# A window-attention and Fourier kernel: the sync queue's transfers moved from a scheduler's order to the program's order

## The chip, the cores and the metric

The kernel runs on one core of a Trainium2 chip. The metric is the device time of one launch in microseconds, the median of several runs. The core has five engines with a queue each: TensorE (PE in the profile; PEld is its weight load), VectorE (DVE), ScalarE (ACT), GpSimd (POOL) and SyncE (SP). In this kernel SP computes nothing. It issues nearly all of the transfers between memory and the on-chip buffers, in the order of its queue, each after the semaphores it waits for.

## The reference

32 images of 56x56 positions and 128 channels, in float32, go through two layers; each is added to its input.

```python
x = x + window_attention(_gn(x), rpb_table, w_qkv, w_proj, b_proj)
x = x + fourier_mlp(_gn(x), w0, w1, W1, b1, W2, b2)
# _gn: normalisation over 32 groups of 4 channels, per image

# window attention: shift by 3, cut into 64 windows of 7x7, 4 heads of 32
qkv  = (win @ w_qkv.T)
attn = softmax(q * scale @ k.T + bias + mask)
out  = (attn @ v) @ w_proj.T + b_proj          # windows back to rows, shift back

# fourier_mlp, 32 modes of 56 along each axis
xy = idct(einsum('bixy,ioy->boxy', dct(x, axis=W)[..., :32], w0))
xx = idct(einsum('bixy,ioy->boxy', dct(x, axis=H)[..., :32], w1))
b  = relu((xx + xy) @ W1 + b1) @ W2 + b2       # 128 -> 512 -> 128
```

## The kernel before, in words

**Cycles.** An image has 8 rows of windows, and the kernel runs in cycles of one such row, 8 to an image. In a cycle it starts the attention of one row (queries, keys, scores), does the values and the projection of the row begun three cycles earlier, and beside these a slice of the Fourier layer of the previous image or of the one before that. `fourier(cycle)` says which slice: the slice numbers c run from 0 to 15 for an image and begin 11 cycles after its first row. Below, i is the number of the cycle modulo 8, so i=0 starts a new image on the attention side.

**Orders.** PE, ACT, DVE and POOL run their instructions as the program writes them: the whole main part stands in a `manual_schedule` over these four. SP is in a second, inner `manual_schedule` only through the prologue (the first image's loads and the first 11 cycles, `first_rows`). In the main loop the scheduler of the library places SP's instructions, by its own estimate of when each can go, among the others.

**Quarters.** The next image comes in as four quarters of 32 rows by 28 columns, called (k, u) in the code. `load_quarter` (lines 145 to 157) issues four DMAs of 112 KB for one; from the third image on all four quarters use one buffer, `xin`. `turn_quarter` (lines 339 to 361) transposes it on DVE (L351, L353, L354 or L356) into the window layout. It is called at the head of a cycle, in `next_quarter`, for (0,0) in i=0, (1,0) in i=4 and (1,1) in i=5; and for (0,1) in the middle of i=0, in `next_groups`. `next_begin` (line 1222), in the second half of a cycle, loads the quarter that the next cycle begins with. The load of (0,1), the "late" one of `next_steps`, stands in `next_quarter` behind the turn of (0,0).

**What follows a turn on DVE.** In i=0 the order on DVE is: sums of the projection's output (L662), turn of (0,0), sums of squares (L683), the copy of the value bias out of PSUM (L433), the even or odd half of the values' output (L622), the two additions of bias and mask to the scores (L506), the row maximum (L516), the turn of an attention block (L575), the turn of (0,1), the row sums (L528, L530), the last addition of the feed-forward (L939), the addition of the projection (L645). PE needs four attention banks `pa` in rotation; L433, L622, L506 and L645 are what frees them, besides ACT.

**The other transfers of the main loop.** Tokens `xr` of a row (`load_tokens`, L132), stores of the attention's result `scr` (L653), columns `htok` (L790), mode stores `zscr` (L813) and mode loads `zT` (`load_modes`, L824, two buffers; called by `load_back` for the next cycle), the residual `res` of a feed-forward group (`ff_in`, L875 and L880, two buffers), which POOL adds a bias to (L892) and DVE adds the result to (L939), and the output (L955, L956, L963, L970).

Of the kernel before, what the change touches and what calls it, by code (L numbers as in the profile page):

```python
# [11 lines left out]
F32 = mybir.dt.float32  # L12
# [4 lines left out]
P = 128  # L17
S = 56
# [3 lines left out]
NH = 4  # L22
HD = C // NH
WT = WS * WS
# [11 lines left out]
JP = 64  # L36
# [9 lines left out]
CONV_BEGIN = NWR + 3  # L46
# [4 lines left out]
def swin_fourier_kernel(  # L51
# [20 lines left out]
    nc = tc.nc  # L72
# [258 lines left out]
    def image_begin(b):  # L331
        im = Image()
        im.b = b
        im.half, im.xw, im.xr, im.eT = {}, {}, {}, {}
        return im
# [27 lines left out]
    def copy_wrap(im, copy):  # L363
        a, b = (
            t[:, : NWR * WS * n].rearrange("p (j h s) -> p j h s", j=NWR, s=WS)
            for t, n in zip((im.half[0], im.half[1]), ROWS)
        )
        copy(b[:, :, KB:], a[:, :, :SS])
# [500 lines left out]
    def ff_in(im, g):  # L869
        t0, n = sum(FF_GROUPS[:g]), FF_GROUPS[g]  # L870
        k, last = n // P, n % P
        xff = im.xf.rearrange("p r w -> p (r w)")
        scr_tok = im.scr.rearrange("h w c -> (h w) c")
        res = work.tile([P, 4, C], F32, tag="res", name="res")
        nc.sync.dma_start(  # L875
            res[:, :k], scr_tok[t0 : t0 + k * P].rearrange("(n p) c -> p n c", p=P)
        )
        if last:
            for hs in HALVES:
                nc.sync.dma_start(res[hs, k, :JP], scr_tok[t0 + k * P : t0 + n, hs])  # L880
        im.res = res
        im.hid = []
        for f in range(NF):
            ph = conv_bank()
            halved(ph[:, :n], wff1[:, f * P : (f + 1) * P], xff[:, t0 : t0 + n])
            hf = work.tile([P, HB], F32, tag="hid", name="hid", bufs=NF)
            nc.scalar.activation(hf[:, :n], ph[:, :n], AF.Relu, bias=b1sb[:, f : f + 1])  # L887
            im.hid.append(hf)
# [135 lines left out]
    def halves_first(cycle):  # L1024
        begins = [im for im, c in fourier(cycle) if c == 0]
        last, j = row(cycle - 4)
        if cycle % NWR == NWR - 1:
            norm_step(cycle)
        tokens_bias(cycle)
        im, i = row(cycle)  # L1030
        behind_short = im and i == NWR - 1
        if behind_short:
            attn_q(im, i)
            attn_exp(cycle - 1)
        if cycle == CONV_BEGIN or (cycle - 1) % NWR not in EARLY:
            divide(cycle)
        if last and cycle > CONV_BEGIN:
            attn_sums(last, j)
        next_quarter(cycle)
        if im:  # L1040
            if not behind_short:
                attn_q(im, i)
            attn_k(im, i)
            if i == NWR - 2:
                wrap_rows(cycle)
        late = im and i in LATE_SQUARES
        if last and cycle > CONV_BEGIN and not late:
            attn_squares(last, j)
            sum_squares(last, j)
        if not late:  # L1050
            next_tokens(cycle)
        if cycle % NWR == 0:
            norm_step(cycle)
        for im, c in fourier(cycle):
            if c in FF_AT:
                ff_in(im, FF_AT.index(c))
        for im in begins:
            start_stats(im)

# [112 lines left out]
    def next_quarter(cycle):  # L1172
        b, quarter, late, _ = next_steps(cycle)
        if quarter:
            turn_quarter(images[b], *quarter)
        if late and (b, *late) not in xins:
            xins[(b, *late)] = load_quarter(b, *late)

# [53 lines left out]
    def first_rows(cycle):  # L1232
        im, i = row(cycle)
        im3, i3 = row(cycle - 3)
        if cycle > 3:
            next_tokens(cycle)
        if im:
            attn_q(im, i)
            attn_k(im, i)
        if cycle == NWR:  # L1240
            norm_step(cycle)
        last, j = row(cycle - 4)
        if last:
            attn_sums(last, j)
        if cycle >= NWR:
            next_quarter(cycle)
        if cycle:
            attn_exp(cycle - 1)
        if im3:
            attn_values(im3, i3, cycle - 3, True)  # L1250
        tokens_bias(cycle)
        if im:
            attn_scores(im, i, cycle)
            attn_max(cycle)
        if last:
            attn_squares(last, j)
            sum_squares(last, j)
            add_sums(last, j)
        divide(cycle)
        turn(cycle)  # L1260
        if im3:
            attn_project(im3, i3)
        if cycle in (0, NWR - 1):
            norm_step(cycle)
        if im:
            attn_v(im, i, cycle)
        if cycle == 0:
            for half in range(2):
                bias_and_mask(nc.vector, 1, 1, half)
        next_begin(cycle)  # L1270
        if cycle < NWR:
            next_quarter(cycle)
        if cycle == NWR - 2:
            wrap_rows(cycle)
        next_groups(cycle)
        if cycle == NWR - 2:
            for _ in range(2):
                norm_step(NWR - 1)
        if cycle in (3, 5):
            back_weights(cycle // 2 - 1)  # L1280
        if cycle == 6:
            ff_weights()
        if cycle == CONV_BEGIN - 1:
            attn_sums(im3, i3)
            attn_squares(im3, i3)
            sum_squares(im3, i3)
            attn_exp(cycle)

    ET = mybir.EngineType
    with tc.manual_schedule(engines={ET.PE, ET.Activation, ET.DVE, ET.Pool}):  # L1290
        with tc.manual_schedule(engines={ET.SP}):
            images[0] = image_begin(0)
            for k in range(2):
                for u in range(2):
                    turn_quarter(images[0], k, u)
                if k:
                    copy_wrap(images[0], nc.vector.tensor_copy)
                for u in range(2):
                    xins[1, k, u] = load_quarter(1, k, u)
                for i in range(NP * k, NP * k + NP):  # L1300
                    row_stats(images[0], i)
            for i in range(2):
                load_tokens(images[0], i)
            for m in range(8):
                mix_weights(m)
            for _ in range(3):
                norm_step(-1)
            for r, t in ((0, 0), (0, 1), (1, 0)):
                for half in range(2):
                    bias_and_mask(nc.vector, r, t, half)  # L1310
            extra = big.tile([P, S, S], F32, tag="xf", name="a_extra", bufs=2)
            extra = extra.rearrange("p r w -> p (r w)")[:, : AT + JP - WT]
            nc.gpsimd.memset(extra[:, AT:], 0.0)
            a_ends.append(extra)
            a_sb.append(extra[:, :AT].rearrange("p (t w j) -> p t w j", t=NH, w=NP))
            for cycle in range(CONV_BEGIN):
                first_rows(cycle)
        for cycle in range(CONV_BEGIN, NB * NWR + CONV_BEGIN + FF_AT[-1] - NWR + 1):
            halves_first(cycle)
            if not row(cycle - 3)[0]:  # L1320
                eighths(cycle)
                for r in range(2):
                    columns_turn(cycle, r)
                behind_max(cycle)
                quarters(cycle)
                last_fetch(cycle)
                half_columns(cycle)
                half_columns(cycle, True)
                scale_first(cycle, 0)
                scale_first(cycle, 1)  # L1330
                load_first(cycle)
                last_out(cycle)
                load_back(cycle + 1)
                continue
            if not has_ff(cycle):
                half_columns(cycle)
            eighths(cycle)
            early = any(c == 10 for _, c in fourier(cycle))
            if early:
                columns_turn(cycle, 0)  # L1340
            quarters(cycle)
            if row(cycle)[0]:
                attn_max(cycle)
            if not early:
                columns_turn(cycle, 0)
            columns_turn(cycle, 1)
            last_fetch(cycle)
            if row(cycle)[0] and cycle % NWR in LATE_SQUARES:
                sum_squares(*row(cycle - 4))
                next_tokens(cycle)  # L1350
            behind_max(cycle)
            load_first(cycle)
            halves_last(cycle)
# [62 lines left out]
```

## Time and profile before

| what | value |
|---|---|
| median of 3 runs | 3230.74 us (3228.96 to 3234.39) |
| the profiled execution, its own time | 3231.41 us |
| its span, first to last instruction | 3229.6 us |
| granted TensorE clock, mean | 0.994 |
| PE / DVE / POOL / ACT busy | 3145.1 / 2517.3 / 2297.7 / 2184.8 us |
| data moved | 448.47 MB, mean 139 GB/s |
| DMA issues of the quarters (`xin`) | 480 of 112 KB |
| DVE idle before L351 for a quarter, 400 to 3000 us | 66.0 us in 51 waits |

A row of the timeline reads: start, duration in us (from the first to the last of merged instructions), engine, line, operation, output<-input with shapes, count, and in brackets the idle time of the engine before it with what ended it. For SP a row is the time in which DMAs are issued; the data land later. A row of the waits reads: engine, line, waited for what, us in total, times, longest. Windows give for a stretch the busy time of each engine, the granted clock, the busy share of the 16 DMA engines and GB/s.

### The profile page before, as it was taken

The page shows a single profiled execution, that of the slowest core. Times are in us where ns is not written, and L with a number is a line of the kernel's source. Part 1 is how long each engine was busy: PE and PEld are TensorE (multiplying, and loading weights), DVE is VectorE, ACT ScalarE, POOL GpSimd, SP SyncE. Part 2 cuts the span into 40 slices and gives each one's busy share as a digit, 9 for nine tenths or more (in the row PEclk, how much of TensorE's full clock was granted, in tenths as well). Part 3 has the DMA queues.
Part 4 walks back from the last instruction along what each step waited for, and adds up shares of the span by engine and source line. Part 5 has one row for each costly group of instructions (what it writes and reads, how often), then busy time and mean ns, then how long its engine had stood idle before and what let it go on. Part 6 is the DMA issues. An engine that isn't in the chain of part 4 may idle for free.

```text
span 3229.6 us, 152033 instructions
## 1 busy us (share of the span) xinstructions
PE 3145.1 (97%) x65664; PEld 2348.3 (73%) x65664; DVE 2517.3 (78%) x4764; ACT 2184.8 (68%) x4004; POOL 2297.7 (71%) x2570
## 2 busy tenths in 40 slices
PE   5789999999999999999999999999999999999999
PEld 4567777777777777777777777777777777777776
DVE  7678887888887888887888887888888888888751
ACT  4466777666777676776676777666776666777664
POOL 5467777777777777777777777777777777777741
PEclk9899999999999999999999999999999999999999
DMA  7446566656566655566656566556656656565443
GB/s 128 96 118 146 140 141 147 140 143 146 136 143 146 144 141 142 141 143 144 144 138 145 140 144 145 143 137 145 143 141 145 148 135 146 143 143 142 123 137 103
DMA packets 1171652, 448.47 MB, mean 139 GB/s; under 512 B 527690, under 2 KB 1141116, under 8 KB 1170980
## 3 DMA queue, kind: packets, MB, share of 16 engines
q1 hardware_dynamic: 1162788, 437.41, 56.9%
q8 instruction: 514, 8.42, 1.2%
q10 hardware_dynamic: 7584, 1.18, 0.3%
q14 instruction: 158, 1.29, 0.1%
q0 software_dynamic: 608, 0.17, 0.0%
HBM read 277.00 MB, written 161.48 MB: 136 GB/s over the span
## 4 chain that ended last, share of the span: by engine, by line
PE 95%; POOL 1%; DVE 1%; ACT 1%; issue 1%; DMA 1%; SPq 0%; DVEq 0%; ACTq 0%; POOLq 0%
PE pc L124 41%; PE pa L124 10%; PE pa L476 8%; PE pc L803 7%; PE pa L498 6%; PE pa L637 6%; PE pa L592 6%; PE pc L842 5%; PE pc L756 4%; PE pc L563 1%; PE pc L929 0%; ACT k L463 0%; PE pa L703 0%; POOL a L517 0%; DMA zT<-zscr 0%
## 5 line engine op out<-in xcount | busy, mean ns | idle before, releaser
L547 POOL TENSOR_TENSOR blocks<-a,rs 32x272 f32<-32x272 f32 (+3 forms) x1434 | 1219.6, 858 | 384.9 <-DVE rs L530 274.6
L124 PE MATMUL pc<-wff,hid 128*64 128x128 f32 x12288 | 713.1, 273 | 1.6 <-issue 0.6
L124 PE MATMUL pc<-xf,wff 128*64 128x512 f32 (+2 forms) x3584 | 714.5, 539 | 0.0
L124 PEld LDWEIGHTS pc<-wff,hid 128*64 128x64 f32 x12288 | 680.0, 137 | 8.4 <-issue 4.2
L517 POOL TENSOR_TENSOR a<-a,mx 128x784 f32<-128x784 f32 x250 | 376.6, 1507 | 294.8 <-DVE mx L516 269.3
L124 PEld LDWEIGHTS pc<-xf,wff 128*64 128x64 f32 x3584 | 263.7, 136 | 370.3 <-issue 295.7
L887 ACT ACTIVATE hid<-pc,b1sb 128x512 f32<-128x512 f32 (+2 forms) x896 | 500.6, 642 | 41.9 <-PE pc L124 41.6
L124 PE MATMUL pa<-xw,wn 128*64 128x392 f32 x2048 | 392.5, 498 | 29.1 <-ACT wn L429 28.5
L506 DVE TENSOR_TENSOR a<-pa,bm 128x392 f32<-128x392 f32 x500 | 259.0, 560 | 168.2 <-PE pa L498 155.5
L483 ACT COPY v<-pa 128x512 f32<-128x512 f32 x256 | 152.0, 594 | 283.7 <-PE pa L476 275.1
L463 ACT ACTIVATE k<-pa,bqkv,heads 128x392 f32<-128x392 f32 x512 | 318.9, 674 | 15.3 <-ACT q L450 1.1
L138 POOL TENSOR_TENSOR xr<-xr,bproj 128x384 f32<-128x384 f32 (+1 forms) x256 | 292.9, 1144 | 47.2 <-DMA xr<-in_x_dram 24.5
L892 POOL TENSOR_TENSOR res<-res,b2sb 128x512 f32<-128x512 f32 (+1 forms) x224 | 252.1, 1126 | 77.7 <-DMA res<-scr 57.1
L778 ACT ACTIVATE y<-modes,rstd 128x448 f32<-128x448 f32 x256 | 276.6, 1138 | 41.8 <-DVE modes L771 31.4
L450 ACT ACTIVATE q<-pa,bqkv 128x392 f32<-128x392 f32 x256 | 149.8, 585 | 229.0 <-PE pa L124 227.2
L523 ACT ACTIVATE a<-a 128x784 f32<-128x784 f32 x250 | 214.0, 856 | 130.3 <-POOL a L517 130.0
L575 DVE STREAM_TRANSPOSE eT<-blocks 128x1024 f32<-128x1024 f32 x240 | 295.1, 1230 | 0.0
L592 PEld LDWEIGHTS pa<-eT,v 49*32 49x32 f32 x16384 | 173.0, 106 | 157.9 <-issue 70.8
L528 DVE TENSOR_REDUCE sm<-a 128x16 f32<-128x784 f32 x250 | 239.8, 959 | 56.0 <-ACT a L523 55.9
L476 PE MATMUL pa<-wn,xw 128*64 128x128 f32 x4096 | 281.8, 279 | 1.6 <-issue 1.2
L516 DVE TENSOR_REDUCE mx<-a 128x16 f32<-128x784 f32 x250 | 242.2, 969 | 7.7
L476 PEld LDWEIGHTS pa<-wn,xw 128*64 128x64 f32 x4096 | 219.8, 137 | 36.6 <-issue 2.3
(126 smaller groups left out, 4978.6 us busy)
## 6 DMA issues: line engine op xcount, KB each, us to landing
zscr<-z SPq DMA_DIRECT2D x512, 112.0 KB
xin<-in_x_dram SPq DMA_DIRECT2D x480, 112.0 KB
htok<-scr SPq DMA_DIRECT2D x128, 392.0 KB
zT<-zscr SPq DMA_DIRECT2D x192, 256.0 KB
res<-scr SPq DMA_DIRECT2D x160, 256.0 KB
out_dram<-res SPq DMA_DIRECT2D x160, 256.0 KB
scr<-x SPq DMA_DIRECT2D x256, 112.0 KB
xr<-in_x_dram SPq DMA_DIRECT2D x256, 84.0 KB
```

The lines of the kernel that those rows point to most:

```text
L124: nc.tensor.matmul(dst[ps], lhsT=lhsT[:, ps], rhs=rhs, start=start, stop=stop)
L138: nc.gpsimd.tensor_tensor(piece, piece, bproj.unsqueeze(1).to_broadcast([P, n, C]), ALU.add)
L463: nc.scalar.activation(k_sb[:, u], pk[:, :RT].rearrange("p (w j) -> p w j", j=WT), AF.Identity, bias=im.bias[:, 3 + u : 4 + u], scale=head ...
L476: nc.tensor.matmul(pv[HALVES[w % 2], w // 2 * C : (w // 2 + 1) * C], lhsT=im.half[i // NP][:, t0 : t0 + JP], rhs=im.w[:, 2 * C : 3 * C], s ...
L506: nc.vector.tensor_tensor(a[:, 2 * hp : 2 * hp + 2, :, 0:WT].rearrange("p u w j -> p w u j"), ps[hp][:, :RT].rearrange("p (w u j) -> p w u ...
L517: nc.gpsimd.tensor_tensor(a3, a3, mx.unsqueeze(2).to_broadcast([P, 2 * NWR, WT]), ALU.subtract)
L547: nc.gpsimd.tensor_tensor(dst[to, k, :, :n], a3[src, :, kb * KB : kb * KB + n], rs[src].unsqueeze(2).to_broadcast([src.stop - src.start, 2 ...
L575: nc.vector.transpose(eT.rearrange("p t (k j) -> p k t j", k=2), blocks[r % 2])
L592: nc.tensor.matmul(po4[u][h * HD : (h + 1) * HD, pr], lhsT=v[ks, pr, h * HD : (h + 1) * HD], rhs=eT[ks, h * NP + pr, :WT], start=True, sto ...
L778: nc.scalar.mul(y[:, r], t.rearrange("p (n k) -> p n k", k=NM), im.rstd)
L887: nc.scalar.activation(hf[:, :n], ph[:, :n], AF.Relu, bias=b1sb[:, f : f + 1])
L892: nc.gpsimd.tensor_tensor(im.res[:, :k], im.res[:, :k], b2sb.unsqueeze(1).to_broadcast([P, k, C]), ALU.add,)
```

## The change

The two blocks of `manual_schedule` become one over all five engines, and the main loop is inside it. So SP runs its transfers in the program's order in the main loop too. The lines of the prologue move one level to the left and are otherwise the same. The load of the late quarter becomes a function of its own, `late_quarter`. In the prologue's cycles it is called where it was; in a cycle of the main loop it is called in `halves_first` behind the loop that issues the residual (`ff_in`).

```diff
@@ halves_first
         for im, c in fourier(cycle):
             if c in FF_AT:
                 ff_in(im, FF_AT.index(c))
+        late_quarter(cycle)
         for im in begins:
             start_stats(im)
@@ next_quarter
         b, quarter, late, _ = next_steps(cycle)
         if quarter:
             turn_quarter(images[b], *quarter)
+
+    def late_quarter(cycle):
+        b, _, late, _ = next_steps(cycle)
         if late and (b, *late) not in xins:
             xins[(b, *late)] = load_quarter(b, *late)
@@ first_rows
         if cycle >= NWR:
             next_quarter(cycle)
+            late_quarter(cycle)
         if cycle:
             attn_exp(cycle - 1)
@@ main part
-    with tc.manual_schedule(engines={ET.PE, ET.Activation, ET.DVE, ET.Pool}):
-        with tc.manual_schedule(engines={ET.SP}):
-            images[0] = image_begin(0)
...
-            for cycle in range(CONV_BEGIN):
-                first_rows(cycle)
+    with tc.manual_schedule(engines={ET.PE, ET.Activation, ET.DVE, ET.Pool, ET.SP}):
+        images[0] = image_begin(0)
...
+        for cycle in range(CONV_BEGIN):
+            first_rows(cycle)
         for cycle in range(CONV_BEGIN, NB * NWR + CONV_BEGIN + FF_AT[-1] - NWR + 1):
             halves_first(cycle)
```

The programs of PE, DVE, ACT and POOL have the same instructions in the same order before and after. SP's queue in the steady part, by cycle (each cycle ends with its `scr` stores; the quarter that an `xin` belongs to is in brackets):

```
i   before                                               after
3   res, xr, htok, out, scr                              xr, res, htok, xin x4 (1,0), out, scr
4   xin (1,1), xr, xin, htok, xin x2, out, scr           xr, res, htok, zT, xin x4 (1,1), out, scr
5   res x2, xr, xin x3 (0,0), out, scr                   xr, res, out, scr
6   zscr x4, xin (0,0), xr, zscr x4, scr                 zscr x4, xr, zscr x4, zT, scr
7   res, zT x2, xr, zscr x4, out, scr                    res, xr, zscr x4, zT x2, xin x4 (0,0), out, scr
0   xin x4 (0,1), xr, zscr x4, zT x2, out, res, scr      xr, res, xin x4 (0,1), zscr x4, zT x2, out, scr
1   res x3, xr x6, xin (1,0), zT x2, xin, out x3, scr    xr x6, res x3, zT x2, out x3, scr
2   xr, res, xin x2 (1,0), zT x2, out x3, scr            xr, res, out x3, scr
```

More of the change, by code (lines that the diff above doesn't have):

```diff
@@ L1289, in swin_fourier_kernel @@
     ET = mybir.EngineType
-    with tc.manual_schedule(engines={ET.PE, ET.Activation, ET.DVE, ET.Pool}):
-        with tc.manual_schedule(engines={ET.SP}):
-            images[0] = image_begin(0)
[L1293 to L1315, printed above, removed]
-            for cycle in range(CONV_BEGIN):
-                first_rows(cycle)
@@ new lines, in swin_fourier_kernel @@
+    with tc.manual_schedule(engines={ET.PE, ET.Activation, ET.DVE, ET.Pool, ET.SP}):
+        images[0] = image_begin(0)
+        for k in range(2):
+            for u in range(2):
+                turn_quarter(images[0], k, u)
+            if k:
+                copy_wrap(images[0], nc.vector.tensor_copy)
+            for u in range(2):
+                xins[1, k, u] = load_quarter(1, k, u)
+            for i in range(NP * k, NP * k + NP):
+                row_stats(images[0], i)
+        for i in range(2):
+            load_tokens(images[0], i)
+        for m in range(8):
+            mix_weights(m)
+        for _ in range(3):
+            norm_step(-1)
+        for r, t in ((0, 0), (0, 1), (1, 0)):
+            for half in range(2):
+                bias_and_mask(nc.vector, r, t, half)
+        extra = big.tile([P, S, S], F32, tag="xf", name="a_extra", bufs=2)
+        extra = extra.rearrange("p r w -> p (r w)")[:, : AT + JP - WT]
+        nc.gpsimd.memset(extra[:, AT:], 0.0)
+        a_ends.append(extra)
+        a_sb.append(extra[:, :AT].rearrange("p (t w j) -> p t w j", t=NH, w=NP))
+        for cycle in range(CONV_BEGIN):
+            first_rows(cycle)
```

## The prediction

> **What bounds the kernel now.** I read the engine table first, then the slices and the chain of waits:
>
> ```profile
> PE 3145.1 (97%) x65664; PEld 2348.3 (73%) x65664; DVE 2517.3 (78%) x4764; ACT 2184.8 (68%) x4004; POOL 2297.7 (71%) x2570
> PE   5789999999999999999999999999999999999999
> PE 95%; POOL 1%; DVE 1%; ACT 1%; issue 1%; DMA 1%; SPq 0%; DVEq 0%; ACTq 0%; POOLq 0%
> ```
>
> TensorE (PE) idles 84.5 us. Busy time by stretches says where: of the first 300 us 69.5 are idle, from 400 to 2800 us 9.1, after 3100 us about 5. In the steady part PE has nothing to give, so anything that makes PE wait lengthens the kernel. What matters is how near VectorE (DVE) is to being late. I took one image, 1600 to 1710 us (i is cycle mod 8; i=0 begins near 1639 us). The sync queue (SP) in order of time at that place:
>
> ```profile
> 1635.28 0.81 SPq L132 DMA_DIRECT2D xr<-in_x_dram  x2
> 1636.43 1.62 SPq L813 DMA_DIRECT2D zscr<-z  x4
> 1641.70 0.40 SPq L963 DMA_DIRECT2D out_dram<-res  x1
> 1642.20 1.26 SPq L653 DMA_DIRECT2D scr<-x  x2
> 1644.54 2.09 SPq L156 DMA_DIRECT2D xin<-in_x_dram  x4
> ```
>
> and DVE, then PE, over the same time:
>
> ```profile
> 1642.18 0.55 DVE L662 TENSOR_REDUCE part<-x 128x32 f32<-128x384 f32 x1
> 1642.67 1.10 DVE L351 STREAM_TRANSPOSE xw<-xin 128x512 f32<-128x512 f32 x1
> ...
> 1644.35 0.50 DVE L683 TENSOR_REDUCE part<-xr 128x32 f32<-128x384 f32 x1
> 1644.76 0.15 DVE L433 COPY bqkv<-pa 128x1 f32<-128x1 f32 x1
> ...
> 1650.41 1.14 DVE L351 STREAM_TRANSPOSE xw<-xin 128x512 f32<-128x512 f32 x1 [1.16 <-DMA xin<-in_x_dram]
> ```
>
> ```profile
> 1644.40 0.81 PE L592 MATMUL pa<-eT,v 49*32 49x49 f32 x64
> 1645.14 0.89 PE L498 MATMUL pa<-k,q 64*49 64x98 f32 x32
> ```
>
> Quarter (0,0) is turned at 1642.67 with no wait before it: its transfers went out in cycles 5 and 6 (1611.13 and 1623.83 us). Behind it on DVE stand L683 and L433, which empties the bank that the second half of the scores (L498) writes: in the program's order that matmul waits for DVE. L433 ends at 1644.9, L498 begins at 1645.14: about 0.3 us of slack.
>
> [...] every instruction stands in the written order, so a late quarter holds L433 and L433 holds PE. [...] From 60 to 160 us (PE 63 to 76% busy) the granted clock is 0.77 to 0.91, from 200 to 300 us (95.5%) 1.00; no run here isolates one gap.
>
> **The change, part by part.** Set against each other, PE, DVE, ACT and POOL keep their instructions in the same order. Only SP's queue moves. Nothing is computed more or less; SP's issue time (0.3 to 0.5 us each) is no bound.
>
> *Quarter (0,0), turned at i=0.* Before: issued 19 to 31 us ahead. After: in the tail of i=7, behind the tokens, four zscr stores and two zT loads. The stores stay where they are, since tokens wait for L683 and stores for ScalarE's copies: they end at 1636.43+1.62=1638.05. In eight images I looked at (380, 767, 1156, 1545, 1642, 1932, 2322, 2709 us) the turn is due 3.5 to 4.75 us after their end, mean 4.2. Two zT issues take 1.05 to 1.5 us, say 1.1: the first quarter DMA goes out 3.1 us before it is due. How long does a quarter take? Quarter (0,1), on which DVE already waits, gives issue-to-turn: 6.00, 5.86, 5.15, 5.89, 5.87, 6.05, 6.07, 5.45. Those have little ahead of them. Quarter (1,1), with htok's 784 KB ahead, took 7.4 to 8.6 us from its last pair. Here 512 KB of zT go ahead, in a stretch where the DMA engines are 0.15 busy now (1639 to 1643 us). I take 6.6. Late by 6.6-3.1=3.5, less 0.3 of slack: PE stands still for 3.2 us in L498. It happens from image 3 to 32, but the first of these lies in the unchanged prologue: 29 times 3.2 = 93 us. Ends: 5.15 gives 1.75 (51 us), 8.0 gives 4.6 (133 us).
>
> *Quarter (0,1), same cycle.* One input buffer, so it waits for the (0,0) turn, now 3.5 us later, and also for tokens and a residual (1.0+0.4 us) that it used to precede. By the same steps: turn ends near 1648.1, L683 1648.5, tokens to 1649.6, residual 1650.0, quarter out at 1650.05, landed at 1655.95 against 1650.41. PE has moved by 3.2 meanwhile. DVE turns until 1657.9, then L528, L530, L939, L645 end at about 1660.4; the next values (L592) want that bank at 1658.10+3.2=1661.3. Covered by about 1 us; if it is gone, PE waits. In i=1 the six token issues (3.45 us) now go ahead of the residual, which lands near the moment GpSimd's bias wants it. I charge 0.5 (0 to 1.5): 29 times = 15 us.
>
> *Quarter (1,0), turned at i=4.* Issued in the tail of i=3 behind htok, about 1681.8 us; with the 7.9 of the htok cases plus two more DMAs, 1690 to 1691.5, wanted at 1690.91. That cycle has DVE idle 0.39 and 1.06 us before L506. Nothing charged; 0.3 if that is gone.
>
> *Quarter (1,1), turned at i=5.* Already late now:
>
> ```profile
>   DMA xin<-in_x_dram: 46.1, 39
>   DMA out_dram<-res: 19.9, 12
> ```
>
> (the idle time of DVE before L351 from 400 to 3000 us, where the second row belongs to the same input: DVE needs no output store here). After: all four DMAs follow htok, and a residual and a zT (512 KB) that used to leave in i=2 and i=3 stand ahead. At 172 GB/s that is up to 3.0 us, I take 2.4. DVE has no idle time from there to L645 in i=5: at 1607.92 to 1618.79 us L645 ends 1.05 us before the next values need its bank (1620.38 against 1619.34). Loss 2.4-1.05=1.35 (0 to 2.2), 30 times = 40 us.
>
> *Residuals and modes.* Residuals go out at the head of their own cycle rather than one ahead. In most cycles POOL's bias stands behind L517 and wants them 2.5 to 7 us later. The zT pair for i=0 leaves at 1638.1 instead of 1630.5, wanted by L842 at 1645.85: covered, and after the change PE arrives 3 us later still. If that cover went, L842 itself would stall; kept in the high end. In the tail a residual no longer leaves before the previous group's output, but it also need not wait for that output to land: 0 to 3 us, taken as 0.
>
> *Sum.* 93+15+40=148. On the profiled execution's span: 3229.6+148=3377.6, plus the 1.8 around it (3231.41 against 3229.6): 3379 us. The profiled execution is 0.7 us from the median 3230.74, so no correction: 3378.
>
> **The rivals.** *Milder:* quarters land as fast as the best seen and only i=0 pays: 29 times 1.2 to 1.75 = 35 to 51 us, 3265 to 3282. For it: the idle DMA stretch. Against: zT's bytes are in that very stretch.
>
> *No change:* another stall absorbs it, or (0,0) is in time. It would have to land within 3.4 us of issue; the shortest of eight is 5.15. 3225 to 3237.
>
> *Faster:* the ramp, where PE is idle 14.2 us in 140 to 230 us, shows PE waiting for DVE's L645 and L683 and for ScalarE's L429. If the old hoisting of transfers causes these, program order could recover at most those 14 plus the 9 of the steady part: 3208 to 3224. It decides only if the quarter at i=0 is not late, that is the same 3.4 us. Against: the waits in the ramp are for compute engines, whose order stays.
>
> *Worse:* [...] zT is late too: up to 3.5 us per image more, 3480.
>
> **How the numbers follow.** My forecast's own range (3290 to 3450): 0.72. Milder 0.11, worse 0.07, no change 0.05, faster 0.05. A measurement of this kernel tells 0.2% (6.5 us) from no change. Both signs: faster 0.05, same 0.05, slower 0.90. Range: from the milder case's middle to the top of mine and a bit of the worse, 3272 to 3465, leaving out about 0.17; the ends follow from 1.75 or less at i=0 alone (51 us and down) and from 4.6+1.5+2.2 (240 us).
>
> **What would show it.** In the changed profile: DVE idle before L351 three to four times larger, mostly at i=0, about 3.5 us per image there; a PE wait before L498 named for DVE's L433 or L354, near 3 us, once per image and new; a smaller one before L592 for L645 or L476 for L622 in i=5 and 6; PE near 93%. The image period rises from about 97 us to 102. If PE shows no wait at L498, the main step is wrong: then the quarter came in time, and the SP order in time would tell. [...]

## The result and the profile after

The changed kernel takes 3464.27 us (median of 4 runs, 3458.83 to 3471.47), beside 3229.85 us (4 runs, 3228.30 to 3234.39) for the kernel before: a ratio of 1.0724, 95% interval 1.0711 to 1.0737, or 234 us more. The forecast was 3378, its range 3272 to 3465. The direction came out as forecast, and so did the place and the cause of the largest wait. That the time lies inside the range, by 0.7 us, is luck: two of the four runs lie above 3465, and the range left next to nothing for the slow clock, which came to some 68 us.

The profiled execution after has a span of 3469.6 us (own time 3471.47). The engine table, PE's slices, the granted clock in the same slices and the chain of work that ended last:

```profile
PE 3224.4 (93%) x65664; PEld 2402.7 (69%) x65664; DVE 2510.3 (72%) x4764; ACT 2184.4 (63%) x4004; POOL 2296.2 (66%) x2570
...
PE   5789999999999999999999999999999999999998
...
PEclk9899999999999999999999999999999999999999
...
PE 66%; SPq 12%; DMA 8%; DVE 8%; issue 3%; POOL 2%; ACT 1%; DVEq 0%; POOLq 0%; ACTq 0%
```

Before, 95% of the chain was PE. Now SP's queue, DMA and DVE together make up 28% of it. The span grew by 240.0 us, and the engine table splits that in two. PE's idle time (span less busy) went from 84.5 to 245.2, so 160.7 us are idle. PE's busy time went from 3145.1 to 3224.4 with the same 65664 matmuls, so the same matmuls were busy 79.3 us longer. Most of that is the clock (0.972 granted in the mean, 0.994 before): counted in the trace, PE is busy for 170.4 us in stretches with half the clock granted, 34.6 before. About half of such time is lost (62 matmuls of L842 take 3.32 us at 607.24, granted 0.50 throughout, and 1.76 at full clock in the run with the short filler). Taken as half, that is 85.2 us against 17.3, so the clock accounts for 67.9 of the 79.3 us; the other 11.4 aren't explained. Both parts have their lines. PE's waits, largest first (engine, line, waited for what: us in total, times, longest):

```profile
PE pa L498 <- DVE bqkv L433: 94.0, 29, 4.9
PE pa L476 <- DVE oT L622: 49.8, 29, 2.9
...
PE pc L842 <- DMA zT<-zscr: 6.5, 4, 3.7
```

The first of these is new (none before). The second had one wait of 0.4 us before. DVE's own wait for the quarters answers to both:

```profile
DVE xw L351 <- DMA xin<-in_x_dram: 353.6, 113, 5.5
```

Before, DVE waited 76.0 us in 57 waits there (53.3 named for these transfers, 22.7 for an output store that the turn doesn't need). By quarter, with a mean over the images from the fourth on, and for (1,1) from the third, DVE stands before the turn for: (0,0) 0.00 before and 3.81 after, (0,1) 1.01 and 3.30, (1,0) 0.00 and 0.53, (1,1) 1.43 and 4.27 us.

The slower matmuls are mostly in two groups (busy us, mean ns of one, then the idle time ahead of them), here before and then after:

```profile
L498 PE MATMUL pa<-k,q 64*49 64x98 f32 x8192 | 231.8, 250 | 5.8 <-ACT k L463 5.8
L842 PE MATMUL pc<-idcth,zT 64*64 64x112 f32 x3584 | 99.2, 256 | 3.2 <-issue 3.1
...
L498 PE MATMUL pa<-k,q 64*49 64x98 f32 x8192 | 256.3, 259 | 99.8 <-DVE bqkv L433 94.0 <-ACT k L463 5.8
L842 PE MATMUL pc<-idcth,zT 64*64 64x112 f32 x3584 | 140.5, 313 | 4.0 <-DMA zT<-zscr 2.4 <-ACT hid L887 0.9 <-issue 0.8
```

Their busy time grew by 24.5 and 41.3 of the 79.3 us. These are the two kinds of matmul that run directly behind the new gap.

**One image, i=0.** SP, DVE and PE in order of time at the place that the prediction showed:

```profile
1742.14 1.66 SPq L813 DMA_DIRECT2D zscr<-z  x4
1743.89 0.95 SPq L824 DMA_DIRECT2D zT<-zscr  x2
1744.90 4.67 SPq L156 DMA_DIRECT2D xin<-in_x_dram  x4
```

```profile
1748.57 0.07 DVE L346 MEMSET xw<- 128x15 f32 x1
1752.47 1.10 DVE L351 STREAM_TRANSPOSE xw<-xin 128x512 f32<-128x512 f32 x1 [3.82 <-DMA xin<-in_x_dram]
...
1754.15 0.49 DVE L683 TENSOR_REDUCE part<-xr 128x32 f32<-128x384 f32 x1
1754.56 0.14 DVE L433 COPY bqkv<-pa 128x1 f32<-128x1 f32 x1
```

```profile
1751.04 0.37 PE L498 MATMUL pa<-k,q 64*49 64x98 f32 x4
1754.76 1.28 PE L498 MATMUL pa<-k,q 64*49 64x98 f32 x26 [3.35 <-DVE bqkv L433]
...
1755.87 2.96 PE L842 MATMUL pc<-idcth,zT 64*64 64x112 f32 x62
```

The quarter goes out behind the zT loads, DVE stands 3.82 us before the turn, L433 comes late behind it, and PE stands 3.35 us in the middle of the scores. Then comes what the sum had left out: L842 takes 2.96 us for 62 matmuls, where 64 took 1.71 before. The windows over the same stretch (busy time of PE, PEld, DVE, ACT, POOL, then granted clock, DMA share, GB/s) show why:

```profile
1751.40:1754.70 3.30, 0.01 (x2) 0.00 (x0) 2.23 (x6) 0.17 (x1) 2.34 (x3) 1.00 0.40 108
1754.80:1756.80 2.00, 2.00 (x50) 2.00 (x54) 1.33 (x5) 0.00 (x0) 0.00 (x0) 0.53 0.35 104
1756.80:1758.80 2.00, 2.00 (x52) 1.85 (x44) 1.97 (x3) 1.13 (x3) 0.73 (x1) 0.62 1.04 216
1758.80:1762.00 3.20, 3.20 (x62) 3.20 (x62) 0.34 (x1) 2.51 (x5) 2.32 (x3) 1.00 0.54 84
```

PE is empty for 3.3 us, and for the 4 us after that it is full but granted 0.53 and 0.62 of its clock.

### The profile page after: what moved, and what is told of

Same layout as the page of the kernel before. It is cut to its first block, busy times and chain, and to the rows that moved or that the text cites. A ratio compares the mean times of both kernels' runs of the same rounds, so it can differ in the third digit from the quotient of the medians.

```text
span 3469.6 us, 151800 instructions
## 1 busy us (share of the span) xinstructions
PE 3224.4 (93%) x65664; PEld 2402.7 (69%) x65664; DVE 2510.3 (72%) x4764; ACT 2184.4 (63%) x4004; POOL 2296.2 (66%) x2570
## 3 DMA queue, kind: packets, MB, share of 16 engines
q14 instruction: 157, 1.28, 0.1%
## 4 chain that ended last, share of the span: by engine, by line
PE 66%; SPq 12%; DMA 8%; DVE 8%; issue 3%; POOL 2%; ACT 1%; DVEq 0%; POOLq 0%; ACTq 0%
PE pc L124 26%; SPq L156 8%; PE pa L124 7%; DMA xin<-in_x_dram 7%; PE pa L476 6%; PE pc L803 6%; PE pa L498 5%; PE pc L842 5%; PE pa L637 4%; PE pa L592 4%; PE pc L756 2%; DVE xw L351 2%; DVE part L683 1%; SPq L132 1%; SPq L824 1%
## 5 line engine op out<-in xcount | busy, mean ns | idle before, releaser
L124 PE MATMUL pc<-wff,hid 128*64 128x128 f32 x12288 | 721.2, 275 | 1.5 <-issue 0.7
L124 PE MATMUL pc<-xf,wff 128*64 128x512 f32 (+2 forms) x3584 | 714.9, 539 | 3.1 <-DVE res L949 2.8
L124 PEld LDWEIGHTS pc<-wff,hid 128*64 128x64 f32 x12288 | 689.7, 139 | 7.0 <-issue 2.7
L124 PEld LDWEIGHTS pc<-xf,wff 128*64 128x64 f32 x3584 | 254.5, 136 | 384.3 <-issue 310.4
L124 PE MATMUL pa<-xw,wn 128*64 128x392 f32 x2048 | 390.1, 497 | 28.2 <-ACT wn L429 27.5
L351 DVE STREAM_TRANSPOSE xw<-xin 128x512 f32<-128x512 f32 x120 | 134.1, 1117 | 353.6 <-DMA xin<-in_x_dram 353.6
L892 POOL TENSOR_TENSOR res<-res,b2sb 128x512 f32<-128x512 f32 (+1 forms) x224 | 251.6, 1123 | 167.4 <-DMA res<-scr 154.8
L498 PE MATMUL pa<-k,q 64*49 64x98 f32 x8192 | 256.3, 259 | 99.8 <-DVE bqkv L433 94.0
L476 PE MATMUL pa<-wn,xw 128*64 128x128 f32 x4096 | 288.0, 284 | 51.0 <-DVE oT L622 49.8
L498 PEld LDWEIGHTS pa<-k,q 64*49 64x49 f32 x8192 | 195.0, 126 | 187.7 <-DVE bqkv L433 99.9
L476 PEld LDWEIGHTS pa<-wn,xw 128*64 128x64 f32 x4096 | 225.9, 140 | 92.3 <-DVE oT L622 56.5
```

What stands on the lines that cost most here:

```text
L124: nc.tensor.matmul(dst[ps], lhsT=lhsT[:, ps], rhs=rhs, start=start, stop=stop)
L476: nc.tensor.matmul(pv[HALVES[w % 2], w // 2 * C : (w // 2 + 1) * C], lhsT=im.half[i // NP][:, t0 : t0 + JP], rhs=im.w[:, 2 * C : 3 * C], s ...
L498: nc.tensor.matmul(ps[hp][e * JP : e * JP + WT, pr * 2 * WT : (pr + 1) * 2 * WT], lhsT=q[cs, w * WT : (w + 1) * WT], rhs=k_sb[cs, :, w], s ...
```

## The experiments

Theory: (0,0) and (1,1) land late because of what the program's order puts ahead of them. Each late quarter costs PE a gap, and behind some of these gaps PE runs at the slow clock besides (0.53 and 0.62 granted in the 4 us behind the one above). The rivals are that the clock falls for another reason, that the residuals, the modes or (0,1) are the cost, and that one written order on SP is a price in itself. This table gathers the runs, with the ratio to the kernel before on the same chip, and span, PE idle and PE busy of the profiled execution.

| run | median, us | ratio, 95% interval | span | PE idle | PE busy |
|---|---|---|---|---|---|
| changed kernel | 3464.27 | 1.0724 [1.0711, 1.0737] | 3469.6 | 245.2 | 3224.4 |
| (0,0) early | 3314.87 | 1.0266 [1.0251, 1.0282] | 3314.2 | 148.9 | 3165.3 |
| (1,1) early | 3419.30 | 1.0585 [1.0569, 1.0601] | 3419.2 | 198.4 | 3220.8 |
| both early | 3276.51 | 1.0151 [1.0135, 1.0167] | 3274.4 | 108.0 | 3166.4 |
| quarters ahead of modes | 3337.74 | 1.0352 [1.0325, 1.0379] | 3333.1 | 154.9 | 3178.2 |
| (0,1) first | 3448.69 | 1.0681 [1.0656, 1.0707] | 3447.3 | 228.4 | 3218.9 |
| gap filled, long | 3460.64 | 1.0727 [1.0707, 1.0747] | 3445.2 | 139.6 | 3305.6 |
| gap filled, short | 3410.38 | 1.0567 [1.0547, 1.0588] | 3416.3 | 155.1 | 3261.2 |
| new function alone | 3230.15 | 1.0008 [0.9999, 1.0017] | 3226.7 | 79.9 | 3146.8 |
| both early, tail | 3259.27 | 1.0090 [1.0075, 1.0106] | 3257.4 | 97.5 | 3159.9 |
| (0,1) first besides | 3260.56 | 1.0109 [1.0089, 1.0129] | 3255.1 | 91.8 | 3163.3 |
| repaired order | 3234.87 | 1.0023 [1.0015, 1.0032] | 3237.3 | 85.3 | 3152.0 |
| repaired, (0,1) last | 3247.53 | 1.0045 [1.0031, 1.0058] | 3244.1 | 95.0 | 3149.1 |

### One quarter early, the other, both

(0,0) is loaded two cycles earlier, in the tail of i=5, when the turn of (1,1) has freed the buffer:

```diff
     def next_begin(cycle):
+        b, quarter, _, _ = next_steps(cycle + 3)
+        if cycle >= CONV_BEGIN and quarter == (0, 0):
+            xins[(b, *quarter)] = load_quarter(b, *quarter)
         b, quarter, _, _ = next_steps(cycle + 1)
```

> The program order of the changed kernel, but quarter (0,0) of the next image is loaded in the tail of cycle i=5, right where its buffer is free, instead of in the tail of i=7. My theory (PE stands still in L498 because DVE is late with quarter (0,0), and the array clock halves after that gap): the wait of L498 for L433 (94 us in 29 times) goes to under 10 us and about 58 us of slow matmuls behind it go too: 3464 - 152 = 3312, between 3295 and 3335. Rival (the loss comes from program order as such: residuals, mode loads and outputs behind SP's long quarter issues, whatever quarter is concerned): less than half of that comes back, over 3390.

Measured: 3314.87, as the theory said. The wait of L498 for L433 is gone, and with it most of the slow clock: busy falls by 59.1 us, idle by 96.3. PE's waits of this run begin so, apart from those of the ramp:

```profile
PE pa L476 <- DVE oT L622: 45.0, 29, 3.9
```

So (0,0) alone is worth 149 us of the 234.

(1,1) is loaded directly behind the turn of (1,0), at the head of i=4:

```diff
         next_quarter(cycle)
+        if im and i == 4:
+            next_begin(cycle)
```

> The changed kernel, but quarter (1,1) is loaded directly behind the turn of (1,0) at the head of i=4, ahead of tokens, residual, htok and zT. My theory: the wait of L476 for L622 (50 us in 30 times) goes, and some 20 us of slow clock behind the longer of these gaps: 3464 - 70 = 3394, between 3375 and 3415; L498's wait for L433 stays at about 94 us. Rival (DMA engines full in i=4 and 5, so that moving one transfer only makes another late): within 20 us of 3464, with a wait of PE for zT or htok in place of the one removed.

Measured: 3419.30, some 4 us above the upper end of what was expected; 45 us came back rather than 70. The wait of L476 for L622 is gone and that of L498 stays:

```profile
PE pa L498 <- DVE bqkv L433: 97.1, 29, 5.4
```

Idle falls by 46.8 us but busy by 3.6 only. The expectation had put some of the slow clock on this gap too, and hardly any of it was there.

Both edits together:

> Both moves together, all other transfers in the changed kernel's program order. My theory: the two late quarters and the clock behind them are the whole loss, so the time is back at 3230 to 3255, with PE busy near 3150 us and granted clock 0.99. Rival (residuals, modes and the late second quarter in program order cost as well): 3280 or more.

Measured: 3276.51, above the expected 3230 to 3255. The two effects add up (149 and 45 make 194; together 188), so they are separate, but 47 us above the kernel before stay. In sum the slow clock is not among them (PE is busy 36.3 us at half clock, 34.6 before). The trace shows one place at once, the rows after the last attention row, where only the Fourier branch runs. SP, then PE:

```profile
3211.77 0.38 SPq L963 DMA_DIRECT2D out_dram<-res  x1
3212.27 1.13 SPq L970 DMA_DIRECT2D out_dram<-res  x2
3213.51 1.06 SPq L824 DMA_DIRECT2D zT<-zscr  x2
```

```profile
3216.64 3.26 PE L842 MATMUL pc<-idctw,zT 64*64 64x112 f32 x64 [3.66 <-DMA zT<-zscr]
```

The mode loads go out behind the output stores, which wait for the last additions. PE stands 3.66 us and then runs L842 at about half speed (3.26 us for 64 matmuls, 1.71 in the image of the kernel before).

### Is the slow clock the gap's doing?

The changed kernel with throwaway matmuls in the place of the gap (in the first row of each image from the third on, ahead of the scores, into the bank that the scores use next). This is extra work; no transfer and no DVE instruction moves. First with seven calls, which are 28 matmuls in the trace:

```diff
         ps = [attn_bank(), attn_bank()]
+        if i == 0 and r > CONV_BEGIN:
+            for _ in range(7):
+                halved(
+                    ps[0][:, :RT].rearrange("p (j t) -> p j t", t=WT), im.w[:, :C], im.xw[i]
+                )
```

> The changed kernel with 14 throwaway matmuls (128x392, about 2.6 us at full clock) in i=0 ahead of the scores, into the bank that the scores overwrite: they run in the time in which PE waits for L433 and keep it busy. Nothing of the result is changed. If the gap is what halves the array clock afterwards: the remaining wait is about 0.7 us, the matmuls behind it run at full speed, and 58 us come back: 3406, between 3390 and 3425, granted clock 0.98 to 0.99. If the slow matmuls have another cause (contention for PSUM or weights from the work that piles up behind the quarter): 3464 within 10 us, with L842 still at 2.8 us and more.

Measured: 3460.64, as good as unchanged, which by itself would speak for the rival. But the filler was mis-sized. It took 4.83 us, not 2.6 (0.17 us for each of the 28), and outlasted the gap:

```profile
1641.63 4.83 PE L124 MATMUL pa<-xw,wn 128*64 128x392 f32 x28
1646.39 0.89 PE L503 MATMUL pa<-k,q 64*49 64x98 f32 x32
```

(The scores are L503 here, five lines further down.) Two things cancelled: idle fell by 105.6 us, and the 30 fillers added 144.1 us to the busy time of L124 (534.2 against 390.1), while busy rose by only 81.2 in all. So the test was repeated with four calls (`range(4)`):

> The changed kernel, with throwaway matmuls in the place where TensorE stands still: in the first row of each image but the first, ahead of the scores, four of 392 columns go into the bank that the scores use next (extra work; the outputs are not changed). In the longer version 28 recorded pieces took 4.83 us, so these 16 should take 2.8 us, less than the stand of 3.2 us. No transfer moves. Theory (the gap itself costs 94 us, and the slow clock behind it some 60 to 80 us more): the stand shrinks to 0.4 to 0.6 us, the clock goes to 0.99, and the 79 us of slow matmuls fall to 10 to 25; 3400 us, between 3385 and 3415. Rival (the slow clock comes from elsewhere, from the slower transfers or the gaps in the sixth row): the clock stays at 0.972 and the time at 3464 within 10 us.

Measured: 3410.38, as the theory said. The filler takes 2.85 us, a wait of L503 for L433 stays in 18 images with 13.7 us in all, and L847 (L842 in the changed kernel) is back at its old speed:

```profile
1622.42 2.85 PE L124 MATMUL pa<-xw,wn 128*64 128x392 f32 x16
...
1626.17 0.80 PE L503 MATMUL pa<-k,q 64*49 64x98 f32 x26 [0.59 <-DVE bqkv L433]
...
1626.82 1.76 PE L847 MATMUL pc<-idcth,zT 64*64 64x112 f32 x62
```

Here DVE waits for (0,0) as in the changed kernel (3.69 us in the mean), the bytes and their order are the same, and still the matmuls behind run at full speed or close to it (L847 with idcth is busy for 104.4 us, 140.5 in the changed kernel and 99.2 before). Idle fell by 90.1 us, the filler added 86.4 to the busy time of L124 (476.5 against 390.1), and busy rose by only 36.8: some 50 us of slow matmuls are gone. The slow clock behind this gap is thus shown to come from PE being empty. It is part of the loss (50 to 63 us by the two fillers, 59 by the early quarter), and the rest of the 79 us lies elsewhere.

### The quarter ahead of the mode loads, and (0,1) first

```diff
         half_columns(cycle, True)
-        load_back(cycle + 1)
         next_begin(cycle)
+        load_back(cycle + 1)
```

> The changed kernel, with the quarter (0,0) issued ahead of the mode loads in the tail, instead of behind them. SP's two mode loads take 0.95 us to issue, so the quarter should land 1 to 2 us earlier and the stand of TensorE before the scores (L498, named L433) should fall from 3.2 us to 1.3 to 2.2 us, once an image. Theory (the lateness of the quarter is all there is, [...]): idle falls by 30 to 55 us, and most of the slow matmuls behind these gaps come back to full speed, another 30 to 50 us; 3395 us, between 3370 and 3420, clock 0.98 to 0.99. Rival (the mode loads are what the kernel needs first): zT then comes late at L842 in every image, some 2 us or more, and the time stays at 3450 or above.

Measured: 3337.74, faster than the theory's 3370. Two lines changed places, and 126 us came back, more than half of the loss. (0,0) comes 1.9 us earlier (DVE waits 1.93 in the mean, not 3.81): its first transfer goes out 4.6 us before the turn is due instead of 3.2, and it then takes 6.35 us to be there instead of 7.0 (medians of 29 images). The gap in the scores falls to 1.46 us in the mean, from 3.24, and the clock is halved behind fewer of them: PE is busy 68.3 us at half clock, not 170.4. What the expectation forgot is that the same two calls stand in the tail of i=4 as well, where a zT load went ahead of (1,1): its wait falls from 4.27 to 2.93 us, and most of that of L476 goes.

```profile
PE pa L498 <- DVE bqkv L433: 40.8, 28, 2.3
...
PE pa L476 <- DVE oT L622: 11.3, 17, 1.3
PE pc L842 <- DMA zT<-zscr: 9.8, 8, 3.6
```

zT, now behind the quarters, costs 3.3 us more in the whole kernel. The rival falls.

Next, the changed kernel with the load of (0,1) directly behind the turn of (0,0), where it was before:

```diff
         next_quarter(cycle)
+        late_quarter(cycle)
         if im:
...
-        late_quarter(cycle)
         for im in begins:
```

> The changed kernel, with the quarter (0,1) issued directly behind the turn of (0,0), ahead of residual, tokens and the mode round trip, as in the kernel before. Theory (the (0,1) quarter is covered, it costs TensorE nothing, and the step of 15 us for it was too much): VectorE's wait for (0,1) falls from 3.3 us to some 1 to 2 us, the time stays at 3464 within 10 us. Rival (the residuals and (0,1) together are a cost of their own): the time falls by 15 us or more.

Measured: 3448.69, 15.6 us less by the medians. By the ratios it is some 14 us, uncertain by 9 from the two intervals, so (0,1) isn't free, which speaks for the rival, but the size isn't settled. DVE's wait for (0,1) falls from 3.30 to 0.81 us. The gain is not where (0,1) is used, though: the waits of L476 for L622 in i=5 went from 49.8 to 38.9 us and those of L498 in the next i=0 from 94.0 to 89.0. One reading is that DVE takes its lateness from i=0 along to the next late quarter; that is argued, not shown.

### The new function without the new order

The kernel before with `late_quarter` split off and called behind the residuals, SP still left to the scheduler:

> The kernel before, with one of the change's two edits alone: the second quarter's load gets its own function and its place behind the residuals, while SP is still left to the scheduler. Theory (the scheduler places SP's transfers by when their buffers come free, whatever line of the program asks first, and the loss is all in the program order): 3229 us, between 3222 and 3240. Rival (the place of the second quarter is a cost of its own): 3245 or more.

Measured: 3230.15, ratio 1.0008 [0.9999, 1.0017]. The scheduler places SP's transfers nearly where it did (DVE's wait for (0,1) grows from 1.01 to 1.92 us, without a loss), and the whole loss is the program order's.

### What a written order could do

The tail first. To both early quarters is added, in the rows after the last attention row:

```diff
                 load_first(cycle)
-                last_out(cycle)
                 load_back(cycle + 1)
+                last_out(cycle)
                 continue
```

> The run with both quarters early (3276.5), with one more line moved: in the rows after the last attention row, the mode loads of the next row are issued ahead of the output stores of this one. Theory (of the 47 us that were left above the kernel before, some 13 are TensorE idle behind zT in these last rows, and the slow clock behind these gaps): the waits at L842 named zT, 8.9 us in 6, go to 1 us or less, and the time falls by 8 to 14 us; 3264, between 3260 and 3270. Rival (the loads are late there because of what comes before them, not because of the stores): 3274 to 3280.

Measured: 3259.27, 17 us less, just below the expected range. The waits for zT fall from 8.9 to 1.6 us.

Then (0,1) directly behind the turn of (0,0) besides, and (1,1) at the end of the head of i=4 rather than behind the turn of (1,0):

```diff
         next_quarter(cycle)
-        if im and i == 4:
-            next_begin(cycle)
+        late_quarter(cycle)
...
-        late_quarter(cycle)
+        if row(cycle)[0] and cycle % NWR == 4:
+            next_begin(cycle)
         for im in begins:
```

> Program order, with every quarter as early as its buffer allows and nothing urgent behind it: (0,0) in the tail of the sixth row, (0,1) directly behind the turn of (0,0), (1,1) in the fifth row behind the tokens and the hidden layer's tokens rather than ahead of them, and the mode loads ahead of the stores in the last rows. Theory (what is left of the loss is (0,1)'s lateness, some 15 us, and the hidden layer's tokens held up behind (1,1), 8 us of slower matmuls): 3243, between 3232 and 3255, and so still not below the kernel before. Rival (the scheduler's order holds nothing that a written order could not have): 3225 to 3231.

Measured: 3260.56, no gain; neither theory's number. DVE now waits for the quarters as little as in the kernel before (0.00, 1.08, 0.29 and 0.17 us), so they are out of it. In particular the wait for (0,1) fell from 3.62 us in the run before to 1.08, and the time did not follow, though (1,1) moved as well. The rest is elsewhere. SP in i=4, and PE behind it:

```profile
1700.92 2.62 SPq L156 DMA_DIRECT2D xin<-in_x_dram  x4
1703.63 1.42 SPq L790 DMA_DIRECT2D htok<-scr  x2
```

```profile
1710.42 0.91 PE L756 MATMUL pc<-htok,dct_h 56*32 56x448 f32 x2
1711.94 0.99 PE L756 MATMUL pc<-htok,dct_h 56*32 56x448 f32 x14 [0.62 <-DMA htok<-scr]
```

The second load of htok still stands behind (1,1), as in the run before: the edit moved (1,1) behind the tokens and the residual only, and not behind htok. The load comes late, and L756 is busy for 143.9 us against 132.1 in the kernel before, with 4.2 us of waits for htok. The second place is the residual: its issue stood behind the tokens, whose load waits on SP until DVE is done with their buffer (373.6 us of such waits for L683). GpSimd then waits 210.2 us for residuals, against 57.1 in the kernel before.

The next order moves these two: (1,1) directly behind the second htok load, the tokens behind the residual.

```diff
         next_quarter(cycle)
         late_quarter(cycle)
...
-        if not late:
-            next_tokens(cycle)
         if cycle % NWR == 0:
...
                 ff_in(im, FF_AT.index(c))
-        if row(cycle)[0] and cycle % NWR == 4:
-            next_begin(cycle)
+        if not late:
+            next_tokens(cycle)
...
                 if c == 1:
                     load_columns(im, 1)
+                    if row(cycle)[0]:
+                        next_begin(cycle)
```

> The last run's order with two transfers moved, by what its trace shows late. (1,1) goes directly behind the second load of the Fourier branch's tokens in the fifth row, not ahead of it (that load, late, held the matmuls of L756 by 15.8 us of longer runs and 5.0 us of waits); and the residuals of the hidden layer go ahead of the next tokens, whose issue waits on SP for VectorE to be done with the buffer (L703 waited 7.7 us behind VectorE, and VectorE behind these residuals). Theory (each of the 26 to 30 us left has a transfer of its own that stands behind a less urgent one): L756 goes back to 168 to 170 us, L703 to 4 us, VectorE waits less than 1.5 us for (1,1); 3236, between 3229 and 3246. Rival (what is left is the price of issuing in one written order at all, each repair pushing the lateness to the next load): 3252 or more.

Measured: 3234.87, as the theory said, with a ratio of 1.0023 [1.0015, 1.0032]. L756 is back at 132.3 us and L703's wait at 4.2; only DVE's wait for (1,1), 2.0 us, is longer than the 1.5 expected. So 227 of the 234 us are back, with SP fully in program order. From 400 to 3000 us PE is idle 8.8 us, as before (9.1). The windows of that stretch (whole row):

```profile
400.00:3000.00 2600.00, 2591.17 (x54146) 1938.53 (x54139) 2117.22 (x3972) 1814.21 (x3325) 1949.99 (x2171) 1.00 0.59 142
```

It doesn't beat the kernel before: some 7 us remain. They aren't in the steady part, where an image takes 96.99 us in both. By 400 us the kernel before has run 7486 matmuls and this one 7400, which is about 4 us at the pace of this stretch (an estimate, from 54064 matmuls in 2600 us before); the rest comes after 3000 us. What holds PE up there isn't settled. Which of the two moves gave how much was not run apart.

The last run takes this order and moves (0,1) back to where the change has it:

> The last run's order with (0,1) moved back to where the change puts it, behind the residual and the tokens; all other transfers stay as early as there. VectorE's wait for (0,1) should rise from 1.3 to some 3.5 us an image. Theory (the 15.6 us that (0,1) was worth in the changed kernel come from the lateness that VectorE carries from it to the next late quarter, and are nothing where the others are in time): 3235, between 3228 and 3242. Rival (the place of (0,1) costs 15 us of its own, wherever the others stand): 3247 to 3254, with a new wait of TensorE in the first or second row.

Measured: 3247.53, ratio 1.0045 [1.0031, 1.0058], against 1.0023 [1.0015, 1.0032]: some 7 us, uncertain by 5, between the theory (nothing) and the rival (15). DVE's wait for (0,1) is 2.85 us instead of 1.23, and the trace shows no named wait of PE that grew by as much. So the place of (0,1) costs something here too. Whether it is less than in the changed kernel the two differences (14, uncertain by 9, and 7, uncertain by 5) don't tell, and where it falls stays open.

## Why the prediction was right, and where not

**(0,0): right, in place and size.** Forecast: a gap of 3.2 us in L498, named for L433, 29 times, 93 us. Measured: 94.0 us in 29, at that line, for that reason. Its terms hold too, as medians over these 29 images: the turn fell due 3.2 us after the first issue (3.1 forecast), and the quarter took 7.0 us from first issue to turn (6.6 forecast; 5.95 to 8.42 measured). The run with (0,0) early shows the cause.

**The clock: the term that was missing.** The sum had no term for it. The prediction left it to the worst of its rivals, with a chance of 7 in 100, and said that no run isolated one gap. Busy time grew by 79.3 us of the 240, 67.9 of them at half clock, and that is most of the miss (3464 - 3378 = 86); the idle time, 160.7 us against 148 forecast, adds 13. After the change, from 300 to 3150 us, the granted clock is at 0.50 for 3.41 or 6.83 us at a time, and one gap of 1.99 us had that behind it. The last section has what the traces show. In four kernels (the changed one, (1,1) early, quarters ahead of modes, (0,1) first), of the gaps at L498 under 1.5 us 1 of 16 was followed by half clock; of those from 1.5 to 2.1 us 7 of 13; from 2.1 to 2.4, 1 of 3; from 2.4 to 3.0, 21 of 25; over 3.0, 56 of 58, with some 1.6 us lost behind each. A forecast gap of 3.2 us stood in the last class, and 29 times some 1.6 us, 46 us, belonged in the sum rather than in a rival.

**(1,1): right in place, low in size.** Forecast 2.4 us later and a loss of 1.35 in i=5, 40 us. (The 172 GB/s behind its 3.0 us is what the kernel before moves from 1695.0 to 1703.6 us, where the 16 engines are 1.04 busy.) DVE waits 2.84 us longer, L476 waits 49.8 us for L622 in 29 waits, 1.72 each. The wait of L592 for L645, which the working used, hardly appears; L476 for L622, named there as the other one, took it all. The run with (1,1) early got back 45 us.

**(0,1): right in size, by a wrong way.** 15 us were charged at L592, and no such wait came. Putting it back is worth some 14 us, uncertain by 9, but through the waits at L476 and L498, and some 7, uncertain by 5, in an order where those are gone.

**Residuals: not covered.** GpSimd's wait for them at L892 rose from 57.1 us in 10 waits to 154.8 in 64, and DVE's wait at L939 for GpSimd from 35.4 to 76.6. What that cost PE in the changed kernel no run separates; the order that puts residuals ahead of tokens is among the two moves that got the last 26 us back.

**SP's issue time "is no bound": wrong.** The issue records of the quarters, 400 to 3000 us (min/median/max in ns of one DMA's issue, first and last start), first the kernel before, then the changed one:

```profile
L156 SPq DMA_DIRECT2D xin<-in_x_dram x424: 321/534/3557, 400.3 to 2957.5; - x142
```

```profile
L156 SPq DMA_DIRECT2D xin<-in_x_dram x395: 317/1068/3692, 399.5 to 2973.0; - x198
```

The median issue takes twice as long, and in the kernel before it was already above the 0.3 to 0.5 us that the prediction took. After, L156 on SP's queue is 8% of the chain that ended last. The four issues of (0,0) take 4.1 us behind the zT loads and 2.9 in the run where they go ahead of them; those of (1,1) take 6.7 us in the changed kernel (medians of 29 images). The prediction counted the bytes ahead of a quarter, but not that SP itself is held up in these issues. What holds it up isn't shown.

**The tail "as 0": wrong.** It looked at residuals and output stores. The mode loads were what came late there; the run that moved them got back 17 us.

**No change, faster, milder:** none of them came, since no quarter (0,0) landed soon enough. The shortest wait for (0,0) is 2.38 us, and the ramp kept its idle time (27.5 us at L124 for L429, as before). DVE's idle time before L351 grew 4.7 times, not three to four. PE at 93% was forecast and came; an image takes 104.8 us, not 102, and 67.9 us of slow clock over 30 images are most of the difference.

## What to carry to other kernels

When an order is written out by hand, list for each queue what each transfer stands behind, and above all what the one ahead of it waits for: here two calls in the wrong order made up half of the loss, and each repair showed the next load in line. Price a new gap on TensorE twice, once as idle time and once for the matmuls behind it: in these traces the second came due behind 1 of 16 gaps below 1.5 us and behind 56 of 58 above 3. And fill a gap with matmuls that change nothing else, if the clock's part is to be told from the wait's; measure the filler first, since one that is longer than the gap hides the answer.

## What the runs showed of the hardware

Two things were not expected. The first is how short a gap of TensorE had half its clock behind it. In the trace of the changed kernel the granted clock is 1.00 or 0.50 throughout, and from 300 to 3150 us it is 0.50 in 33 stretches, 24 of them 3.41 us long and 9 of them 6.83. All 33 begin inside a gap of PE at L498 (26 of the 27 gaps there) or at L476 (7 of the 26 gaps over 0.8 us there), or within 1.4 us of its end. The length of a gap alone doesn't tell: one of 2.68 us (at L476, before 2561.20) cost no clock, and one of 1.99 us (at L476, before 2454.20) was followed by half clock. What decides it isn't shown. The windows around the two (busy time of PE, PEld, DVE, ACT, POOL, granted clock, DMA share, GB/s), first the longer gap, then the shorter one:

```profile
2557.79:2561.20 3.41, 0.73 (x33) 0.52 (x25) 2.90 (x7) 0.00 (x0) 0.00 (x0) 1.00 0.47 124
2561.20:2564.61 3.41, 3.41 (x62) 3.41 (x64) 3.38 (x6) 1.63 (x2) 0.91 (x1) 1.00 0.49 144
2564.61:2568.02 3.41, 3.41 (x50) 2.55 (x48) 3.41 (x6) 2.75 (x5) 2.12 (x3) 1.00 0.02 5
...
2451.24:2454.65 3.41, 1.42 (x52) 1.21 (x42) 3.36 (x8) 0.00 (x0) 0.00 (x0) 1.00 0.29 73
2454.65:2458.06 3.41, 3.41 (x36) 3.41 (x34) 3.38 (x7) 1.63 (x2) 1.36 (x1) 0.50 0.49 143
2458.06:2461.47 3.41, 3.41 (x60) 3.16 (x58) 3.38 (x7) 2.24 (x3) 1.67 (x3) 1.00 0.02 5
```

The matmuls show such a stretch too: at half speed the time lost is half of the time taken. Behind the gap at 1754.76 the 26 scores lost 1.28-0.80=0.48 us and the 62 matmuls of L842 lost 2.96-1.76=1.20 against the run with the short filler, and twice the sum is 3.4. The granted clock is 0.50 there from 1754.91 to 1758.32, for 3.41 us.

The second is that the time that SP takes to issue four DMAs of 112 KB is not a constant. The medians of 29 images are 2.1 us for (0,1) before, 4.1 for (0,0) in the changed kernel and 2.9 for it where the zT loads come behind, and one set behind htok took 7.78 us (1793.32, changed kernel).
